# Single rows per step in a graph layer's gather: 80 by SP and 84 by ScalarE, instead of 76 by each

## The chip, the cores and the metric

The kernel runs on one core of a Trainium2 chip. The metric is the device time of one execution in microseconds (us). A core has five engines with instruction streams of their own: TensorE (PE in the profile), VectorE (DVE), ScalarE (ACT), GpSimd (POOL) and SyncE (SP). ACT, SP and POOL can also issue DMA transfers; the profile shows the issues as rows of ACTq, SPq and POOL.

## The reference

One layer of a graph network over 50,000 nodes with 128 features and 1,650,000 edges, sorted by destination. An edge has a type, 0 or 1, and each type has its own weight matrix and bias.

```
Xs    = X[src]
msg   = where(edge_type == 0, Xs @ W_data.T + b_data, Xs @ W_control.T + b_control)
agg   = segment_sum(msg, dst)
out   = relu(agg + X @ W_self.T + b_self)
x_new = layernorm(x + out)
```

All of it is computed in float32. The expensive part is `X[src]`: 1,650,000 rows of 512 bytes, in an order that only the input knows.

## The kernel before, in words

**Blocks and steps.** The edge list is cut into blocks. A block owns a window of nodes (B = 124) and has Q = 2 steps. The kernel sums the rows `X[src]` per destination and type first, and applies the weights afterwards, once per block. The sum is a product on TensorE: for up to 128 gathered rows, a 0/1 matrix `oh` made from the destinations and types says to which column each row is added.

**Three kinds of rows.** A step has R = 14 gathers of 128 rows, which POOL issues as indirect DMAs (function `gathers`, L551). Beside them it has S = 76 "single" rows: each is a plain DMA of 512 bytes whose address was loaded into a register (function `single_rows`). SP issues the single rows of a block's first step (q = 0), ACT those of its second step (q = 1). The registers are loaded up to LOAD = 28 at a time: 28, 28 and 20 (L580), and then come a register move and a DMA for each row (L585). F = 53 further edges a step fill places in the gathers' lists. So a block takes 14 x 2 x 128 + 2 x (53 + 76) = 3842 edges, and there are 430 blocks. The first and the last block are "plain": they have gathers alone. Single rows exist for blocks 1 to 428. The last block holds what is left over, 2050 edges in 17 gathers.

**What sets the order.** The order is written out by hand in the loop over blocks at the end of `straight`. In iteration b the single rows of block b + FAR (FAR = 4) are issued. They land in one of ten buffers (`y1`, five for each queue), so step q of block b + 4 can't start before TensorE has used step q of block b - 1. The gathers of a step land in one of SLOTS = 5 buffers. SP also stores each finished block (L691), loads the edge lists of ten blocks at a time (L196 to L200) and, for every eighth block, a window of transposed node features (L490). ACT also computes a square root for two blocks at once (L677).

**Marks.** Every queue sets 14 marks in a step's single rows, evenly spread: after row k it has set (k + 1) * 14 // 76 of them (L530, a semaphore that is counted up). `pace` holds POOL back by them: gather k of block b, from block 4 on, waits until queue k % 2 (0 is SP, 1 is ACT) has set k // 2 marks of its step for block b + 1 (LAG = 1). A block without single rows after it is not held back.

```
for k in ks:
    pace(b, k)
    ...
    copy = nc.gpsimd.indirect_dma_start(
```

**Products.** TensorE waits for a step's gathers (L558), multiplies them (L607), waits for the step's single rows (L611) and multiplies those in one more product (L613). DVE makes `oh`, counts, fills and the normalisation, and turns the single rows' indices into byte addresses (`offsets`, L191) for ten blocks at once.

Of the kernel before, what the change touches and what calls it, by code (L numbers as in the profile page):

```python
# [33 lines left out]
R = 14  # L34
W = 64
Q = 2
# [3 lines left out]
F = 53  # L40
LATE = 10
FX = LATE + F
R1 = R + 1
# [2 lines left out]
SIZES = [P] * R  # L46
SIZE = sum(SIZES)
CE = Q * SIZE
S = 76
LOAD = 28  # L50
BE = CE + Q * (F + S)
NBLK = 2 + (E + LATE - CE) // BE
REST = E + LATE - CE - (NBLK - 2) * BE
REST_ROWS = [min(n, max(0, REST - q * SIZE - sum(SIZES[:r]))) for q in range(Q) for r, n in enumerate(SIZES)]
# [28 lines left out]
TBL = GROUPS * GB  # L83
# [8 lines left out]
def plain(b):  # L92

    return b == 0 or b >= NBLK - 1
# [6 lines left out]
def straight(ctx, tc, c, x, x_t, edges_t, edges_f, edges_1, dst_first, first_p, out):  # L101
# [13 lines left out]
    nc = tc.nc  # L115
# [73 lines left out]
    def offsets(g):  # L189
        off = eds.tile([GB * Q, S], I32, name="off")  # L190
        nc.vector.tensor_scalar(off, one_g.pop(g), float(ROW), float((N - 1) * ROW), op0=ALU.mult, op1=ALU.min)  # L191
        off_g[g] = off

    def load_edges(g):
# [3 lines left out]
        nc.sync.dma_start(f.rearrange("b m f -> b (m f)"), edges_f[g * GB:(g + 1) * GB, :])  # L198
        one = eds.tile([GB * Q, S], I32, name="sd1", bufs=1)
        nc.sync.dma_start(one, edges_1[g * GB * Q:(g + 1) * GB * Q, :])  # L200
# [249 lines left out]
    def chunks_of(b, q):  # L450

        n = RCH if b == NBLK - 1 else C if b < NBLK else 0
        return range(q * R, max(q * R, min((q + 1) * R, n)))

    def column(k):
        return k // R * R1 + k % R

    def steps_of(b):
        return [q for q in range(Q) if len(chunks_of(b, q))]
# [12 lines left out]
    ys, ohs, cnts, accs, xTs, pos, hs, mvs, sds, os_ = {}, {}, {}, {}, {}, {}, {}, {}, {}, {}  # L472
# [54 lines left out]
    issued_no, asked, marks = [0] * Q, [0] * Q, {}  # L527

    def mark(q):
        (nc.scalar if q else nc.sync).sem_inc(issued[q], 1)  # L530
        issued_no[q] += 1
# [12 lines left out]
    def gathers(b, ks):  # L544
        i = pass_no[0] % SLOTS
        pass_no[0] += 1
        y = gat.tile([P, R, D], F32, name="y")
        for k in ks:
            pace(b, k)
            r = REST_ROWS[k] if b == NBLK - 1 else SIZES[k % R]  # L550
            copy = nc.gpsimd.indirect_dma_start(  # L551
                out=y[:r, k % R, :].bitcast(U8), out_offset=None, in_=x_rows,
                in_offset=bass.IndirectOffsetOnAxis(ap=idxs[b][:r, column(k):column(k) + 1], axis=0))
            copy.then_inc(landed[i], 16)
            tc.no_tile_sem_insts.add(copy.ins.name)
            tc.add_to_no_dep_group(f"rows{b}_{ks[0]}", copy.ins)
        seen[i] += 16 * len(ks)
        wait = nc.tensor.wait_ge(landed[i], seen[i])  # L558
        tc.declare_fence(wait.ins, group=f"rows{b}_{ks[0]}")
        return y  # L560
# [3 lines left out]
    got = [0] * ALONE  # L564
# [3 lines left out]
    def single_rows(b):  # L568
        if plain(b):
            return  # L570
        g, i = divmod(b, GB)
        for q in range(Q):
            j = alone_no[0] % ALONE
            alone_no[0] += 1
            marks[b, q] = issued_no[q]
            y = one.tile([S, D], F32, name="y1")
            for s0 in range(0, S, LOAD):
                n = min(LOAD, S - s0)
                at = i * Q + q
                _, regs = nc.values_load_multi_w_load_instructions(  # L580
                    off_g[g][at:at + 1, s0:s0 + n], engines=[ACT if q else SP], min_val=0, max_val=(N - 1) * ROW,
                    skip_runtime_bounds_check_because=CLAMPED)
                for k, r in enumerate(regs):
                    r = nc.s_assert_within(r, 0, (N - 1) * ROW, skip_runtime_bounds_check_because=CLAMPED)
                    copy = (nc.scalar if q else nc.sync).dma_start(y[s0 + k:s0 + k + 1, :].bitcast(U8),  # L585
                                               x_bytes[bass.ds(r, ROW)].rearrange("(p e) -> p e", e=ROW))
                    copy.then_inc(alone[j], 16)
                    tc.no_tile_sem_insts.add(copy.ins.name)
                    tc.add_to_no_dep_group(f"single{b}_{q}", copy.ins)
                    while issued_no[q] - marks[b, q] < (s0 + k + 1) * R // S:  # L590
                        mark(q)
            got[j] += 16 * S
            singles[b, q] = y, alone[j], got[j]

    def products(b, q, ks):
        of_step = chunks_of(b, q)
        if b == NBLK - 1:
            ys[b, q] = gathers(b, ks)
        elif ks[0] == of_step[0]:
            ys[b, q] = gathers(b, of_step)  # L600
        y = ys[b, q]
        if ks[0] == 0:
            accs[b] = ps.tile([P, Q, 3, W], F32, name="acc")
        acc = accs[b][:, q]
        for k in ks:
            r = REST_ROWS[k] if b == NBLK - 1 else SIZES[k % R]
            nc.tensor.matmul(acc[:, :2, :].rearrange("p t w -> p (t w)"), y[:r, k % R, :], ohs[b][:r, column(k), :],  # L607
                             start=k == of_step[0], stop=k == of_step[-1] and plain(b))
        if ks[-1] == of_step[-1] and not plain(b):
            y, landed_1, n = singles.pop((b, q))  # L610
            wait = nc.tensor.wait_ge(landed_1, n)  # L611
            tc.declare_fence(wait.ins, group=f"single{b}_{q}")
            nc.tensor.matmul(acc[:, :2, :].rearrange("p t w -> p (t w)"), y, ohs[b][:S, q * R1 + R, :], start=False, stop=True)  # L613
        if ks[-1] == of_step[-1] and q == steps_of(b)[-1]:
            for t in range(2):
                nc.tensor.matmul(accs[b][:, :q + 1, 2, :], to_row[:, t, :], cnts[b][:, :q + 1, t * W:(t + 1) * W],  # L616
                                 start=t == 0, stop=t == 1)
# [107 lines left out]

    columns(0)
    single_rows(1)
    spread(1)
    fill(1)
# [13 lines left out]
    for b in range(2, FAR):  # L743
        single_rows(b)
    made, fresh = 2, [2]
    ready = []
    for b in range(NBLK):
# [23 lines left out]
        if b == NBLK - 1:  # L771
            layer(b - 1)
            moments(b - 1)
            root(pair(b - 1))
            own_part(b)
            store(pair(b - 1))
            for done in pair(b - 1):
                store_rows(done)
            for step, ks in passes_of(b):
                if ks:  # L780
                    products(b, step, ks)
            break
# [3 lines left out]
        if b + FAR < NBLK:  # L786
            single_rows(b + FAR)
        for q, (step, ks) in enumerate(passes_of(b)):
            if ks:
                products(b, step, ks)  # L790
# [28 lines left out]
    b = NBLK - 1  # L819
# [340 lines left out]
```

## Time and profile before

| | |
|---|---|
| median of 3 runs | 15066.82 us (15066.48 to 15069.68) |
| the profiled execution, its own time | 15065.38 us |
| its span, first to last instruction | 15063.7 us |
| busy: PE, DVE, POOL | 39%, 80%, 76% of the span |
| POOL's gathers | 12012 + 17 |
| single rows on SP and on ACT | 32528 each |
| mean DMA rate | 61 GB/s |

Busy shares leave out register moves, semaphore instructions and DMA issues on SP and ACT. In the groups' rows, the part before the bar names line, engine, operation, tiles, shapes and count; then come busy time in us and the mean of one in ns; then the engine's idle time just before them and what ended most of it. In the waits' rows stand the total in us, how often, and the longest. In the timeline's rows stand the start in us from the span's start and the duration of a merged group of like instructions, with their count after the x; in brackets is the idle time before it.

### The profile page before, as it was taken

Reading aid. Unit: us, or ns where it says so; the run is one execution under the profiler, and the core shown is the slowest. Engines: PE = TensorE matmul, PEld = TensorE weight load, DVE = VectorE, ACT = ScalarE, POOL = GpSimd, SP = SyncE. Lnnn points to the kernel's source line nnn. Section 1 sums busy time; section 2 is a strip of 40 time slices with the busy share of each in tenths; the row PEclk is TensorE's granted clock in tenths of the full one; section 3 lists DMA queues with packets and bytes.
Section 4 is the critical chain, followed back from the end, with each engine's and each line's share of the span. In section 5 each row is a group of like instructions: output and inputs, shape, how many; then the busy total and the mean of one; then the engine's idle time right before and its main releaser. Section 6 shows DMA issues by size and latency. Waiting matters only on the chain. (4 is left out here: it accounts for less than half of the span.)

```text
span 15063.7 us, 244090 instructions
## 1 busy us (share of the span) xinstructions
PE 5857.4 (39%) x32862; PEld 5479.9 (36%) x32863; DVE 12073.6 (80%) x11957; ACT 67.2 (0%) x222; POOL 11376.7 (76%) x12039
## 2 busy tenths in 40 slices
PE   3433333333333333333333333333333333333333
PEld 3333333333333333333333333333333333333333
DVE  9878888877877788888888887878788888887875
ACT  0000000000000000000000000000000000000000
POOL 7777777777777777777777777777777777777777
PEclk7666666666666666666666666666666666666666
DMA  2222222222222222222222222222222222222222
GB/s 64 60 62 60 61 61 60 62 60 61 62 60 60 62 60 60 62 60 60 61 60 60 63 60 60 61 60 62 60 60 62 60 60 61 60 61 62 60 59 57
DMA packets 588595, 914.45 MB, mean 61 GB/s; under 512 B 262747, under 2 KB 381952, under 8 KB 586944
## 3 DMA queue, kind: packets, MB, share of 16 engines
q0 software_dynamic: 384928, 789.04, 20.8%
q1 hardware_dynamic: 136522, 92.72, 2.4%
q10 hardware_dynamic: 65494, 16.98, 0.6%
q14 instruction: 1384, 11.34, 0.2%
q8 instruction: 267, 4.37, 0.1%
HBM read 870.39 MB, written 27.30 MB: 60 GB/s over the span
## 5 line engine op out<-in xcount | busy, mean ns | idle before, releaser
L551 POOL DMA_INDIRECT y<-in_x,idx x12012 | 11359.3, 946 | 3667.3 <-issue 3075.1
L607 PE MATMUL acc<-oh,y 128*128 128x128 f32 x24058 | 4774.6, 384 | 8916.1 <-PEq L558 8871.1
L607 PEld LDWEIGHTS acc<-oh,y 128*128 128x128 f32 x24058 | 4571.4, 293 | 9247.8 <-issue 5053.0
L515 DVE TENSOR_REDUCE cnt<-oh 128x256 bf16<-128x3840 f32 x430 | 2834.7, 6592 | 14.7
L507 DVE TENSOR_TENSOR oh<-col,small 128x3840 f32<-128x3840 f32 x430 | 1781.5, 4143 | 0.0
L416 DVE TENSOR_REDUCE by<-new 128x126 bf16<-128x1890 f32 x428 | 1497.0, 3498 | 14.6
L621 DVE TENSOR_TENSOR sums<-acc,sums 128x192 f32 x860 | 307.3, 357 | 1341.1 <-PE acc L616 1292.9
L395 DVE COPY small<-cb 128x30 f32<-128x30 f32 x428 | 82.0, 192 | 1219.7 <-PE small L423 1219.7
L400 DVE TENSOR_TENSOR new<-m,small 128x1890 f32<-128x1890 f32 x428 | 909.0, 2124 | 14.7
L397 DVE TENSOR_TENSOR m<-rk,small 128x1890 f32<-128x1890 f32 x428 | 908.9, 2124 | 14.6
L404 DVE TENSOR_REDUCE v_new<-new 128x30 f32<-128x1890 f32 x428 | 907.9, 2121 | 14.7
L413 DVE TENSOR_TENSOR new<-m,small 128x1890 f32<-128x1890 f32 x428 | 905.8, 2116 | 0.0
L613 PE MATMUL acc<-oh,y 76*128 76x128 f32 x1712 | 334.0, 276 | 0.0
L651 PE MATMUL po<-wmsgT,sums 128*124 128x128 f32 x1720 | 304.5, 300 | 0.0
L613 PEld LDWEIGHTS acc<-oh,y 76*128 76x128 f32 x1712 | 265.6, 195 | 0.0
L641 PE MATMUL po<-own_w,xT 128*124 128x256 f32 x860 | 262.3, 386 | 0.8 <-DVE h L657 0.8
L637 DVE TENSOR_TENSOR sums<-pl,sums 128x372 f32<-128x372 f32 x428 | 233.2, 545 | 14.9
L651 PEld LDWEIGHTS po<-wmsgT,sums 128*124 128x124 f32 x1720 | 221.5, 188 | 53.0 <-issue 1.6
L448 DVE TENSOR_TENSOR pl<-pl,xT 128x248 f32<-128x248 f32 x428 | 181.7, 425 | 46.6 <-DVE xT L501 2.7
L649 PE MATMUL po<-bias,sums 3*124 3x128 f32 x860 | 208.3, 322 | 1.2 <-DVE sums L621 1.2
L649 PEld LDWEIGHTS po<-bias,sums 3*124 3x124 f32 x860 | 125.2, 183 | 149.3 <-issue 147.4
L501 DVE COPY xT<-xw 128x124 f32 x430 | 111.7, 260 | 77.4 <-issue 74.2
(147 smaller groups left out, 2915.1 us busy)
## 6 DMA issues: line engine op xcount, KB each, us to landing
y<-in_x SPq DMA_DIRECT2D x32528, 0.5 KB
y<-in_x ACTq DMA_DIRECT2D x32528, 0.5 KB
y<-in_x,idx POOLq DMA_INDIRECT x12012
xw<-in_x_t SPq DMA_DIRECT2D x54, 496.0 KB
out<-o SPq DMA_DIRECT2D x430, 62.0 KB
sdt<-in_edges_t SPq DMA_DIRECT2D x43, 450.0 KB
sdt_f<-in_edges_f SPq DMA_DIRECT2D x43, 14.8 KB
sd<-in_edges SPq DMA_DIRECT2D x43, 5.9 KB
```

Source lines behind the costliest of these rows:

```text
L397: nc.vector.tensor_tensor(m, rk_g[g][:, i, :, None].to_broadcast([P, C1, FX]), rank_no_ps[:, None, :].to_broadcast([P, C1, FX]), op=ALU.is ...
L400: nc.vector.tensor_tensor(new.rearrange("p (q r) f -> p q r f", r=R1), m.rearrange("p (q r) f -> p q r f", r=R1), vf.rearrange("p (q f) -> ...
L404: nc.vector.tensor_reduce(v, new, AX.X, ALU.add)
L413: nc.vector.tensor_tensor(old, m, cb[:, :, None].to_broadcast([P, C1, FX]), op=ALU.mult)
L416: nc.vector.tensor_reduce(by, old.rearrange("p (q r) f -> p q f r", r=R1), AX.X, ALU.add)
L507: nc.vector.tensor_tensor(oh, col_g[g][:, i, :, None].to_broadcast([P, C1, 2 * W]), num_ps[:, None, :].to_broadcast([P, C1, 2 * W]), op=AL ...
L515: nc.vector.tensor_reduce(cnt, ohs[b].rearrange("p (q r) w -> p q w r", r=R1), AX.X, ALU.add)
L551: copy = nc.gpsimd.indirect_dma_start(out=y[:r, k % R, :].bitcast(U8), out_offset=None, in_=x_rows, in_offset=bass.IndirectOffsetOnAxis(ap ...
L607: nc.tensor.matmul(acc[:, :2, :].rearrange("p t w -> p (t w)"), y[:r, k % R, :], ohs[b][:r, column(k), :], start=k == of_step[0], stop=k = ...
L613: nc.tensor.matmul(acc[:, :2, :].rearrange("p t w -> p (t w)"), y, ohs[b][:S, q * R1 + R, :], start=False, stop=True)
L649: nc.tensor.matmul(po, a[0:3, 2, :B], bias, start=False, stop=False)
L651: nc.tensor.matmul(po, a[:, t, :B], c["wmsgT"][:, t * D:(t + 1) * D], start=False, stop=t == 1)
```

## The change

The number of single rows becomes one for each step, SINGLE = (80, 84): 80 in a block's first step, on SP, and 84 in its second, on ACT. Each step still loads its registers in three loads, 28, 28 and 24 on SP, 28, 28 and 28 on ACT, and each still sets 14 marks. The buffer of a step has room for 84 rows, and the product takes as many of them as were filled. A block takes 3584 + 106 + 164 = 3854 edges, so there are 429 blocks, and the last one has 768 edges in 6 gathers, all of its first step. The host lays out the edge list to match.

```diff
-S = 76
-LOAD = 28
-BE = CE + Q * (F + S)
+SINGLE = (80, 84)
+LOADS = (28, 28)
+S = max(SINGLE)
+BE = CE + Q * F + sum(SINGLE)
...
-            for s0 in range(0, S, LOAD):
-                n = min(LOAD, S - s0)
+            for s0 in range(0, SINGLE[q], LOADS[q]):
+                n = min(LOADS[q], SINGLE[q] - s0)
...
-                    while issued_no[q] - marks[b, q] < (s0 + k + 1) * R // S:
+                    while issued_no[q] - marks[b, q] < (s0 + k + 1) * R // SINGLE[q]:
                         mark(q)
-            got[j] += 16 * S
+            got[j] += 16 * SINGLE[q]
...
-            nc.tensor.matmul(acc[:, :2, :].rearrange("p t w -> p (t w)"), y, ohs[b][:S, q * R1 + R, :], start=False, stop=True)
+            nc.tensor.matmul(acc[:, :2, :].rearrange("p t w -> p (t w)"), y[:SINGLE[q], :], ohs[b][:SINGLE[q], q * R1 + R, :], start=False, stop=True)
```

More of the change, by code (lines that the diff above doesn't have):

```diff
@@ L1122 @@
         rest = a[CE:].reshape(TBL - 1, BE)
-        steps = rest.reshape(TBL - 1, Q, SIZE + S + F)
+        step_at = [sum(SIZE + s + F for s in SINGLE[:q]) for q in range(Q)]
         cols = np.full((TBL, Q, R1, P), pad, np.int32)
@@ L1127 @@
             cols[0, :, r, :n] = a[:CE].reshape(Q, SIZE)[:, at:at + n]
-            cols[1:, :, r, :n] = steps[:, :, at:at + n]
+            for q in range(Q):
+                cols[1:, q, r, :n] = rest[:, step_at[q] + at:][:, :n]
             cols[NBLK - 1, :, r, :n] = rest[NBLK - 2, :CE].reshape(Q, SIZE)[:, at:at + n]
-        cols[1:NBLK - 1, :, R, :S] = steps[:NBLK - 2, :, SIZE:SIZE + S]
+        for q, n in enumerate(SINGLE):
+            cols[1:NBLK - 1, q, R, :n] = rest[:NBLK - 2, step_at[q] + SIZE:][:, :n]
         if k == "src":
@@ L1133 @@
         fills = np.full((TBL * Q, FX), pad, np.int32)
-        own = steps[:NBLK - 2, :, SIZE + S:].reshape((NBLK - 2) * Q, F)
+        own = np.stack([rest[:NBLK - 2, step_at[q] + SIZE + n:][:, :F] for q, n in enumerate(SINGLE)], 1).reshape(-1, F)
         fills[Q:(NBLK - 1) * Q, LATE:] = own
```

## The prediction

> **What bounds the kernel now.** I read the page's costliest groups first, for an engine that has no slack, then the waits of that engine, then its timeline.
>
> ```profile
> span 15063.7 us, 244090 instructions
> PE 5857.4 (39%) x32862; PEld 5479.9 (36%) x32863; DVE 12073.6 (80%) x11957; ACT 67.2 (0%) x222; POOL 11376.7 (76%) x12039
> L551 POOL DMA_INDIRECT y<-in_x,idx x12012 | 11359.3, 946 | 3667.3 <-issue 3075.1
> ...
> POOL y L551 <- issue: 3079.1, 10088, 0.3
> POOL y L551 <- ACTq L530: 254.6, 834, 0.3
> POOL y L551 <- SPq L530: 228.4, 748, 0.3
> ...
> 7000.10 0.94 POOL L551 DMA_INDIRECT y<-in_x,idx  x1 [0.30 <-issue]
> 7001.35 0.94 POOL L551 DMA_INDIRECT y<-in_x,idx  x1 [0.31 <-SPq L530]
> ...
> 15048.96 0.88 POOL L551 DMA_INDIRECT y<-in_x,sdt  x1 [0.30 <-issue]
> ```
>
> By busy share DVE (80%) stands above POOL (76%), but POOL has no idle time that is a wait: each of its gathers takes 0.94 us, 0.30 us passes before the next, and the longest idle time before one is 0.3 us, whoever is named as the releaser. So POOL runs gather after gather from start to end. There are 28 x 429 + 17 = 12029 of them, from about 3 us to 15048.96: 15046 / 12028 = 1.249 us each, 28 x 1.249 = 34.97 us a block. That is the period everything else must stay under. The last gather ends at 15049.8, and 13.9 us of work follow.
>
> ACT and SP look empty (ACT 0%), because DMA issues are not counted as busy. But POOL's gathers wait on marks that these queues set, so how full the queues are has to be read from their timelines. First ACT's queue, in three stretches: before any result is stored, early, and late.
>
> ```profile
> 80.44 30.27 ACTq L585 DMA_DIRECT2D y<-in_x  x76
> ...
> 145.42 0.47 ACTq L585 DMA_DIRECT2D y<-in_x  x1
> ...
> 408.33 63.71 ACTq L585 DMA_DIRECT2D y<-in_x  x152
> 472.22 0.29 ACT L677 ACTIVATE sd<-mv,eps 124x2 f32<-124x2 f32 x1 [65.72 <-issue]
> 474.33 65.80 ACTq L585 DMA_DIRECT2D y<-in_x  x152
> 540.31 0.29 ACT L677 ACTIVATE sd<-mv,eps 124x2 f32<-124x2 f32 x1 [67.80 <-issue]
> ...
> 676.06 24.02 ACTq L585 DMA_DIRECT2D y<-in_x  x57
> ...
> 13070.36 0.29 ACT L677 ACTIVATE sd<-mv,eps 124x2 f32<-124x2 f32 x1 [69.80 <-PEq L558]
> 13078.23 62.26 ACTq L585 DMA_DIRECT2D y<-in_x  x152
> ```
>
> 152 rows are two steps of 76. From 408.33 to 676.06 ACT does eight steps, 33.47 us each, and after each ACTIVATE the next row comes 2.1 us later. Late, the row after the ACTIVATE comes 7.6 us later (13070.66 to 13078.23): there ACT waits. So early ACT runs freely at 33.47 us a step, gains 34.97 - 33.47 = 1.5 us a block on POOL, and stops gaining once it is as far ahead as its ten row buffers let it be. From 80.44 to 145.42 are two quieter steps, 32.49 us each. ACT's whole reserve is therefore 1.5 us a block in the busy stretch and 2.5 us in the quiet one.
>
> SP's queue, early and late, and the wait that holds it back late:
>
> ```profile
> 371.33 29.90 SPq L585 DMA_DIRECT2D y<-in_x  x76
> 401.45 0.28 SPq L691 DMA_DIRECT2D out<-o  x1
> 403.91 30.05 SPq L585 DMA_DIRECT2D y<-in_x  x76
> ...
> 671.78 28.29 SPq L585 DMA_DIRECT2D y<-in_x  x70
> ...
> 13087.69 0.28 SPq L691 DMA_DIRECT2D out<-o  x1
> 13094.17 29.91 SPq L585 DMA_DIRECT2D y<-in_x  x76
> ...
> SPq L585 <- PE acc L613: 803.6, 340, 4.0
> ```
>
> From 371.33 to 671.78 SP does nine steps, 33.38 us each, its store of a block's result included. Late it waits for PE to release a row buffer: 803.6 us in all.
>
> **The change part by part.** A block takes 3584 + 106 + 164 = 3854 edges instead of 3842. That leaves 429 blocks, and the last has 768 edges, six gathers instead of 17. *Removed:* POOL issues 28 x 428 + 6 = 11990 gathers, 39 fewer; at 1.249 us that is 48.7 us off the engine that sets the end now. The edges do not vanish: they become eight more rows on ACT and four more on SP in every block.
>
> What a row and a register load cost on ACT, from one quiet step:
>
> ```profile
> 103.86 6.85 ACTq L585 DMA_DIRECT2D y<-in_x  x20
> L585 ACTq DMA_DIRECT2D y<-in_x x32528: 227/228/617, 15.3 to 14891.8; - x200
> ...
> L580 ACTq TENSOR_LOAD <-off x1: 1949/1949/1949, 90.1 to 90.1; - x1
> L580 ACTq TENSOR_LOAD <-off x1: 1538/1538/1538, 102.2 to 102.2; - x1
> ```
>
> Twenty rows took 6.85 us, the first of them 0.47 us as in the row at 145.42; the others (6.85 - 0.47) / 19 = 0.336 us each, register move and marks included. Bounds: 0.32 with the marks taken out (their number, 14 a step, stays), 0.36 if the busy stretch's slower rows are added. Eight rows: 2.7 us (2.6 to 2.9). The third load of a step brings 20 registers in 1.54 us now, the second 28 in 1.95 us. With 84 rows all three bring 28, so the third grows by 0.41 us. Together ACT's step grows by 3.1 us (3.0 to 3.3).
>
> Of loads, the Trainium skill ("DMA: Bandwidth & Descriptors", Latency and other measured facts) says that a `tensor_load` has a floor of about 600 ns, and names no slope. If a load cost a flat sum, the term of 0.41 us would be nothing and the step 3.1 - 0.4 = 2.7 us longer; the two loads above differ with their width, so I keep the term.
>
> SP's step grows by 4 x 0.336 and, for 24 registers instead of 20, half of 0.41 us: 1.55 us. Freely running that is 33.38 + 1.55 = 34.9 us, just under POOL's 34.97: SP by itself would still keep up.
>
> ACT would not: 33.47 + 3.1 = 36.6 us a step by the busy stretch, 32.49 + 3.1 = 35.6 by the quiet one, and both are over 34.97. The cover that hid ACT's issues is used up by 0.6 to 1.6 us a block. What is late next is POOL: a gather of block b with odd number waits for a mark of ACT's step for block b + 1. At the start there is no lead to live on. Block 4, the first with these waits, begins on POOL after 112 gathers, at about 143 us, and ACT's step 5 began at 145.42. So ACT paces POOL from block 4 to block 426, and a block lasts as long as ACT's step.
>
> Between 35.6 and 36.6 I take 36.0. Early, SP's rows follow its store by 2.46 us (401.45 to 403.91) and rows on both queues are slower; late, SP waits and they follow by 6.5 us (13087.69 to 13094.17). With ACT as the bound, SP, needing 34.9 or less, soon runs as far ahead as its buffers go and waits a little over a microsecond after each store. That is less than late in the kernel before, so part of the slowness should stay.
>
> The sum: ACT's first row of step 5 stood at 145.42 us; four steps grown by 3.1 put it at 157.8. Steps 5 to 427 are 423 periods. Their last odd gather is released some 4.3 us before the end of the last period (the next step's load that isn't there, 2.3, and the rows behind the last but one mark, 2.0). After it POOL has one gather of block 426, 28 of 427 and 6 of 428, which wait for no mark: 35 x 1.249 = 43.7. Then the 13.9 us of the end, and the 1.7 us that the profiled execution (15065.4 us) had outside its span: 157.8 + 423 x 36.0 - 4.3 + 43.7 + 13.9 + 1.7 = 15440.8 us. In general 212.8 + 423 x step. The profiled execution lies 1.4 us below the median of the runs, which is nothing here.
>
> Costed at nothing: the rows' products on PE and the scaling of the offsets on DVE.
>
> ```profile
> L613 PE MATMUL acc<-oh,y 76*128 76x128 f32 x1712 | 334.0, 276 | 0.0
> L607 PE MATMUL acc<-oh,y 128*128 128x128 f32 x24058 | 4774.6, 384 | 8916.1 <-PEq L558 8871.1
> L191 DVE TENSOR_SCALAR off<-sd 20x76 int32<-20x76 int32 x43 | 8.0, 187 | 0.1
> ```
>
> A product of 76 rows takes 0.276 us against 0.384 for 128 rows, so 84 rows cost at most 0.11 more; PE idles 8916 us in front of its gathers' products. The scaling runs 43 times at 0.19 us, eight columns more, on a DVE that POOL does not wait for. Uncovered, both would be under 0.5 us a block.
>
> **The rivals.** *POOL stays the bound* (the other side: faster). Only the 39 gathers count: 15065.4 - 48.7 = 15016.7 us. It decides if ACT's step of 84 stays at 34.97 or less. For it: POOL never waits for ACT today, and late ACT idles visibly. Against it: eight rows and the wider load would have to cost 1.5 us (busy) or 2.5 us (quiet) instead of 3.1.
>
> *The step lands within 0.1 us of POOL's period*: the lost and the won time cancel, about 15065 us, a step of 35.1. Nothing but chance speaks for it.
>
> *ACT as quiet as before the first store*: 35.25 to 35.7 (the low end is 32.49 + 8 x 0.32 + half of the load's 0.41), so at 35.6 the end is 212.8 + 423 x 35.6 = 15272 us. For it: the late stretch of the kernel before, where 152 rows take 62.26 us with waits inside. *ACT as busy as from 408 to 676 us throughout*: 212.8 + 423 x 36.6 = 15695 us. For it: in that stretch ACT also ran without a wait, which is what it will do.
>
> *One descriptor generator for both queues.* If a row held something shared for all of its 0.228 us, a block's 164 rows would need 37.4 us and the end would be 212.8 + 423 x 37.4 = 16033 us. Against it: 152 rows at 0.228 are 34.7 us, yet both queues did a step in 33.4 us, loads included, so rows overlap. The Trainium skill ("Perfetto Trace Analysis", DMA Instruction — HWDGE) says that the generator is locked for exclusive use within the profiled time of such a DMA; by these rows the lock can hold only a part of it.
>
> **How the numbers follow.** ACT's step between 35.7 and 36.4 us: 0.48, at 36.0, 15441 us. Quiet, 35.25 to 35.7: 0.25. Busy, 36.4 to 36.9: 0.14. Shared generator: 0.03. POOL stays the bound: 0.08. Cancelled: 0.02. The range takes the quiet and the busy case in, from a step of 35.25 (15124) to 36.65 (15716). Within 0.2%, 30 us, a run can't be told from no change. Faster 0.08, same 0.02, slower 0.90.
>
> **What would show it.** If I am right, POOL's waits for ACT's marks (254.6 us in all, longest 0.3) become several hundred microseconds with single ones of some microseconds. The row after every ACTIVATE comes about 2 us later, late in the run too. SP still waits for PE at its rows. The last ACT row, 157 us ahead of the last gather before (14891.8 to 15048.96), comes some 45 us ahead of it. 28 gathers take 36 us in mid-run. I am wrong if POOL's longest wait stays at 0.3 us and the last gather starts near 15000 us; the slope is wrong if ACT's rows, freely running, take other than 0.32 to 0.36 us or its 28-register loads other than 1.95 us.

## The result, and the profile after

The changed kernel takes 36,611.95 us (median of 4 runs, 36,607.55 to 36,614.29) against 15,066.65 us before: 2.43 times as long, 95% interval 2.4258 to 2.4342. The forecast was 15,441 us.

The costliest groups on the page of the changed kernel:

```profile
span 36612.5 us, 357556 instructions
L991 POOL DMA_INDIRECT y<-table,idx x14000 | 14921.6, 1066 | 5919.8 <-issue 2757.7
L994 PE MATMUL pa<-y,oh 128*125 128x128 f32 x28000 | 11037.7, 497 | 7973.5 <-DMA y<-table,idx 7938.8
L552 POOL DMA_INDIRECT y<-in_x,idx x11984 | 11323.0, 945 | 4191.5 <-issue 2990.2
```

The gathers of before are there, now as L552. Two of the three costliest groups did not exist before: 14,000 gathers from a `table` and 28,000 products. They belong to a function `general`, which computes the whole layer a second time, from a table of messages per node. The kernel has always held it, behind a branch that the text above has not spoken of. `find_bad` finds, on the chip, whether anything in the input doesn't fit the fast layout, and the branch asks for what it found:

```
nc.vector.tensor_scalar(bad[:, 2:3], latest, float(LATE), None, op0=ALU.is_gt)
nc.vector.tensor_scalar(bad[:, 0:1], mm[:, 0:1], 0.0, None, op0=ALU.is_lt)
nc.vector.tensor_scalar(bad[:, 1:2], mm[:, 1:2], float(W), None, op0=ALU.is_ge)
...
found = nc.values_load(bad, min_val=0, max_val=4 * P,
...
with tc.If(found > 0):
    ...
    general(own, tc, c, x, src, dst, etype, out)
```

The third line is the one that matters here: a step's destinations have to lie within W = 64 nodes, counted from the step's first one (0 to 63 above it). Where the one computation ends and the other begins is in the timeline of POOL, and the share of each in the table by stage (busy time of each engine, then TensorE's granted clock, DMA share and GB/s):

```profile
15523.19 0.94 POOL L552 DMA_INDIRECT y<-in_x,sdt  x1 [0.30 <-issue]
15530.19 0.24 POOL L851 IOTA node<- 128x125 f32 x1 [6.06 <-PE po L652]
...
0.00:15534.00 15534.00, 6034.14 (x32765) 5451.42 (x32766) 12045.14 (x11933) 66.74 (x221) 11333.93 (x12006) 0.64 0.28 59
15534.00:36612.00 21078.00, 11582.59 (x30373) 7324.99 (x30373) 2872.24 (x3883) 188.53 (x646) 14941.98 (x14014) 0.51 0.20 52
```

So the first computation, the one that the forecast is about, ends near 15,534 us, and 21,078 us come on top. In the first one the waits, the issues and ACT's timeline look like this:

```profile
POOL y L552 <- ACTq L531: 873.4, 1218, 2.2
POOL y L552 <- SPq L531: 258.8, 846, 0.7
...
L586 ACTq DMA_DIRECT2D y<-in_x x35868: 234/235/610, 15.9 to 15480.8; - x200
L581 ACTq TENSOR_LOAD <-off x1281: 1875/2012/2214, 13.8 to 15469.1; - x183
...
448.82 70.20 ACTq L586 DMA_DIRECT2D y<-in_x  x168
...
669.46 30.48 ACTq L586 DMA_DIRECT2D y<-in_x  x72
...
13132.68 0.29 ACT L678 ACTIVATE sd<-mv,eps 124x2 f32<-124x2 f32 x1 [72.44 <-issue]
13134.78 70.04 ACTq L586 DMA_DIRECT2D y<-in_x  x168
```

POOL now waits for ACT's marks: 873.4 us in all, up to 2.2 us at once. Before, no idle time that the profile put down to ACT's marks was longer than the 0.3 us that pass between any two gathers. After the end of the ACTIVATE the next row comes 1.8 us later, late in the run too (13132.97 to 13134.78; before it was 7.6 us). From the first to the last row ACT does 427 steps in 15,465 us, 36.2 us each. It sets the pace.

### The profile page after: what moved, and what is told of

It is laid out like the page before. It is cut to its first block, busy times and chain, and to the rows that moved or that the text cites. A ratio compares the mean times of both kernels' runs of the same rounds, so it can differ in the third digit from the quotient of the medians.

```text
span 36612.5 us, 357556 instructions
## 1 busy us (share of the span) xinstructions
PE 17616.7 (48%) x63138; PEld 12776.4 (35%) x63139; DVE 14917.4 (41%) x15816; ACT 255.3 (1%) x867; POOL 26275.9 (72%) x26019
## 5 line engine op out<-in xcount | busy, mean ns | idle before, releaser
L991 POOL DMA_INDIRECT y<-table,idx x14000 | 14921.6, 1066 | 5919.8 <-issue 2757.7
L994 PE MATMUL pa<-y,oh 128*125 128x128 f32 x28000 | 11037.7, 497 | 7973.5 <-DMA y<-table,idx 7938.8
L552 POOL DMA_INDIRECT y<-in_x,idx x11984 | 11323.0, 945 | 4191.5 <-issue 2990.2
L994 PEld LDWEIGHTS pa<-y,oh 128*125 128x125 f32 x28000 | 6916.8, 308 | 12088.2 <-DMA y<-table,idx 11608.3
L608 PEld LDWEIGHTS acc<-oh,y 128*128 128x128 f32 x23980 | 4355.2, 282 | 9649.1 <-issue 8223.5
L1013 DVE TENSOR_TENSOR acc<-pa,bself 125x128 f32<-125x128 f32 x400 | 116.7, 292 | 17208.3 <-PE pa L994 17208.3
L608 PE MATMUL acc<-oh,y 128*128 128x128 f32 x23980 | 4646.7, 375 | 3461.6 <-PEq L559 3460.9
L516 DVE TENSOR_REDUCE cnt<-oh 128x256 bf16<-128x3840 f32 x429 | 2869.6, 6689 | 14.6
L987 DVE TENSOR_TENSOR oh<-rel,node 128x4375 f32<-128x4375 f32 x400 | 1883.3, 4708 | 1.7
L387 PE MATMUL small<-v_f,row_of 74*128 74x126 bf16 x427 | 106.8, 251 | 3097.5 <-DVE at L431 3061.1
L417 DVE TENSOR_REDUCE by<-new 128x126 bf16<-128x1890 f32 x427 | 1498.5, 3509 | 14.6
L684 DVE RECIPROCAL rstd<-sd 124x2 f32<-124x2 f32 x215 | 35.7, 166 | 3076.9 <-ACT sd L678 3076.9
L398 DVE TENSOR_TENSOR m<-rk,small 128x1890 f32<-128x1890 f32 x427 | 907.2, 2125 | 14.6
L401 DVE TENSOR_TENSOR new<-m,small 128x1890 f32<-128x1890 f32 x427 | 907.0, 2124 | 14.7
L405 DVE TENSOR_REDUCE v_new<-new 128x30 f32<-128x1890 f32 x427 | 906.1, 2122 | 14.7
L1007 PE MATMUL px<-ident,x_g 125*128 125x125 f32 x400 | 139.3, 425 | 1207.1 <-DMA t<-in_edge_type 458.8
L614 PE MATMUL acc<-oh,y 80*128 80x128 f32 (+1 forms) x1708 | 405.0, 326 | 0.0
```

Of the source, the lines that this page charges most:

```text
L398: nc.vector.tensor_tensor(m, rk_g[g][:, i, :, None].to_broadcast([P, C1, FX]), rank_no_ps[:, None, :].to_broadcast([P, C1, FX]), op=ALU.is ...
L401: nc.vector.tensor_tensor(new.rearrange("p (q r) f -> p q r f", r=R1), m.rearrange("p (q r) f -> p q r f", r=R1), vf.rearrange("p (q f) -> ...
L405: nc.vector.tensor_reduce(v, new, AX.X, ALU.add)
L417: nc.vector.tensor_reduce(by, old.rearrange("p (q r) f -> p q f r", r=R1), AX.X, ALU.add)
L516: nc.vector.tensor_reduce(cnt, ohs[b].rearrange("p (q r) w -> p q w r", r=R1), AX.X, ALU.add)
L552: copy = nc.gpsimd.indirect_dma_start(out=y[:r, k % R, :].bitcast(U8), out_offset=None, in_=x_rows, in_offset=bass.IndirectOffsetOnAxis(ap ...
```

## The experiments

Two things had to be told apart: what started the second computation, and whether the first one by itself behaves as forecast. Counting over the input's destinations, with 3854 edges a block, finds edges outside in one place only: the last eleven of the edges that fill places in block 7's first step all go to one node, 64 above the step's first node, where 63 is the last that fits. (The expectations below speak of one edge; it is one node, with eleven edges.) With 3842 edges there is none. All other conditions hold in both. That count was made off the chip; the runs test it.

**Moving the edges by 50 places.** Empty places at the end of the first block's list shift all later blocks by 50 edges. By the count no edge is outside then.

```diff
+PADS = 50
...
+        a = np.concatenate([a[:CE - PADS], np.full(PADS, pad, np.int32), a[CE - PADS:]])
```

> The changed kernel with 50 empty places put at the end of the first block's list, so that every later block begins 50 edges later; the instructions stay the same but for one gather more in the last block. Theory A (one filled edge of block 7 lies 64 nodes above its step's first node, the check for the 64-node window counts it, and the whole layer is computed a second time): no edge lies outside now, so 15,525 to 15,555 us, the 15,533 us at which the first computation ends in the changed kernel and little else. Theory B (another check trips, or the second computation has another cause): 36,612 us as before.

Measured: 20,034 us, beside 19,464 us for the kernel before in the same set of runs: ratio 1.0301 (1.0284 to 1.0319). The second computation is gone, there is no L991 in the profile. But the kernel before was 4,400 us slower than it had been. The waits and issues of this run show where (last, the register moves of the kernel before in the first profile):

```profile
POOL y L553 <- SPq L532: 4297.7, 2012, 5.2
...
L587 SPq MOVE y<-in_x x34160: 2/29/1403, 15.8 to 19925.1; - x200
...
7029.73 43.19 SPq L587 DMA_DIRECT2D y<-in_x  x80
...
L585 SPq MOVE y<-in_x x32528: 29/29/37, 15.2 to 14874.6; - x200
```

A register move on SP takes 29 ns at the median and at most 37 ns in the first profile; here single ones take up to 1,403 ns, and 80 rows of SP take 43 us instead of 31 to 32. Both queues stood still at times, at any instruction. Below, "standing queues" means this. In such a set a ratio says what an edit does to the second computation, but the price of rows can't be read from it.

**The kernel before, with its edges moved by 34 places.** By the count this puts two edges of block 7 at 64 nodes there too.

> The kernel before, 76 rows in both steps, with 34 empty places put at the end of the first block's list; by the input, a filled edge of block 7 then lies 64 nodes above its step's first node. Theory A: the second computation runs here too, 15,067 + (36,612 - 15,533) = 36,146 us, between 36,120 and 36,170. Theory B (it takes 80 and 84 rows): 15,067 us.

Measured in the same set, in one run: 42,210 us, 22,745 us more than the kernel before, where 21,079 us more were expected; the queues stood in this run too. The second computation runs, with 76 rows in both steps:

```profile
L991 POOL DMA_INDIRECT y<-table,idx x14000 | 14748.5, 1053 | 7776.4 <-issue 3462.0 <-remote 1347.6 <-DMA s<-in_src 1089.5
...
POOL y L552 <- SPq L531: 4163.0, 2116, 6.8
```

So it doesn't take 80 and 84 rows; it takes edges outside the window.

**The check's limit at 65 nodes.** One constant of the changed kernel is another:

```diff
-nc.vector.tensor_scalar(bad[:, 1:2], mm[:, 1:2], float(W), None, op0=ALU.is_ge)
+nc.vector.tensor_scalar(bad[:, 1:2], mm[:, 1:2], float(W + 1), None, op0=ALU.is_ge)
```

> The changed kernel with one constant changed: the check for the window counts an edge as outside from 65 nodes on instead of 64. It leaves out that one edge's proper column (it is added for the wrong type). Theory A: 15,525 to 15,550 us. Theory B, another check: 36,612 us.

Measured in the same set, in one run: 20,000.9 us beside 19,464 us, and no second computation. So no other condition of `find_bad` was met, and no edge lies further out than 64. With the two runs above, that settles the cause of the factor 2.43.

> The changed kernel with the window check's limit at 65 nodes instead of 64 and nothing else, sent alone; it leaves out the proper column of one edge. The first computation of the changed kernel ended at 15,533 us of its trace. If that is what it takes by itself, 15,525 to 15,555 us beside a kernel before of 15,067 us, ratio 1.031, and POOL's waits for ACT's marks as in the changed kernel (873 us in all). If the added rows cost nothing once the second computation is gone: 15,018 us. If the queues stand still in the kernel before too: about 1.02 to 1.03 of it.

The same kernel in a later set without standing queues, beside a kernel before of 15,072 us: 15,535.4 us (15,531 to 15,544), ratio 1.031 (1.0293 to 1.0327). This is the first computation by itself. Its waits, issues, last gathers and the ACT queue, early and late:

```profile
span 15529.7 us, 253706 instructions
...
POOL y L552 <- ACTq L531: 793.1, 1042, 2.5
SPq L586 <- PE acc L614: 378.9, 152, 3.6
...
L586 ACTq DMA_DIRECT2D y<-in_x x35868: 227/228/631, 15.9 to 15470.5; - x200
L552 POOL DMA_INDIRECT y<-in_x,sdt x6: 940/943/945, 15506.9 to 15513.1; - x6
...
445.58 70.33 ACTq L586 DMA_DIRECT2D y<-in_x  x168
...
664.66 34.24 ACTq L586 DMA_DIRECT2D y<-in_x  x84
...
13053.54 71.04 ACTq L586 DMA_DIRECT2D y<-in_x  x168
...
13271.61 3.45 ACTq L586 DMA_DIRECT2D y<-in_x  x10
```

Six steps from 445.58 to 664.66 take 36.5 us each, six from 13053.54 to 13271.61 take 36.3; over all 427 steps it is 36.2.

**68 rows by SP, 84 by ACT.** The blocks, the 12,029 gathers and the edges per block are those of the kernel before.

```diff
-SINGLE = (80, 84)
+SINGLE = (68, 84)
```

> 68 rows by SP and 84 by ACT: 3842 edges a block as in the kernel before, so the same 430 blocks and 12029 gathers; eight rows only change queues. If ACT's step of 84 rows sets the pace: 212.8 + 424 x step + 11 x 1.249, which is 15,279 us at 35.5 us a step (SP, with fewer rows, waits longer after its stores and leaves ACT's rows quiet) and 15,533 us at 36.1 (ACT's rows as slow as in the changed kernel, whatever SP does). If POOL stays the bound: 15,067 us.

> 68 rows by SP, 84 by ACT, the blocks and gathers of the kernel before. Without the stalls: 15,279 us if ACT's step falls to 35.5 us with SP waiting longer after its stores, 15,533 us if it stays at 36.1 us whatever SP does, 15,067 us if ACT's rows don't set the pace at all.

Both of these were measured with standing queues: 1.0206 (1.0181 to 1.023) and 1.0237 (1.0217 to 1.0258) of the kernel before.

> 68 rows by SP and 84 by ACT again, with the blocks and gathers of the kernel before. In the last two sets of runs the queues of SP and ACT stood still for 0.7 us and more at a time, in the kernel before as well (19,464 and 19,632 us). If the kernel before takes 15,067 us here: 15,279 us if ACT's step falls to 35.5 us because SP waits longer after its stores, 15,533 us if ACT's step stays at 36.1 us whatever SP does, 15,067 us if ACT doesn't set the pace. If the queues stand still here too, about 1.02 to 1.03 of the kernel before.

> 68 rows by SP and 84 by ACT once more: the earlier run gave 15,254 us in its profiled execution and 15,506 us in its other one. If SP's waiting after its stores settles how slow ACT's rows are, and either course can set in, single executions fall near 15,254 us (ACT's step 35.4 us) or near 15,506 us (36.0 us), and in a trace of the second kind SP's first row follows its store sooner than in a trace of the first (9 us and 2.5 us by turns there). If 15,506 us was a single disturbance: all near 15,254 us.

In two sets without standing queues the kernel before took 15,066 and 15,083 us, and this one 15,254 us, then 15,247 to 15,304 us (ratio of the second set 1.0131, 1.011 to 1.0151). In each of the two sets one further execution took 15,506 and 15,503 us; what it did inside is not known, because the traces kept are of 15,254 and 15,247 us, so the question of the last expectation stays open. In the first of these POOL, ACT and SP did this:

```profile
POOL y L552 <- ACTq L531: 455.9, 946, 1.6
...
13058.88 68.72 ACTq L586 DMA_DIRECT2D y<-in_x  x168
...
13270.90 4.33 ACTq L586 DMA_DIRECT2D y<-in_x  x12
...
7034.97 0.28 SPq L692 DMA_DIRECT2D out<-o  x1
7044.37 26.73 SPq L586 DMA_DIRECT2D y<-in_x  x68
```

Six steps from 13058.88 to 13270.90: 35.3 us each, a microsecond less than above with the same 84 rows on ACT; over the whole run it is 35.4 against 36.2. SP has twelve rows fewer. Here it waits up to 9.4 us after its store before its next row, but that is no difference: the mean from store to next row is 4.0 us in both traces. What differs is ACT's rows right after SP's store. From 400 us on, and with the register loads left out, they start 0.380 us apart on the mean in the first 10 us after a store beside 80 rows of SP, and 0.345 beside 68; in the remaining time it is 0.347 in both. Some 20 rows of a step fall into those 10 us, so this makes 0.7 of the 0.8 us. Moving eight rows from SP to ACT thus costs 1.3%, with not one gather saved or added: POOL was no longer what set the end.

**The changed kernel with its edges moved, again.**

> The changed kernel with 50 empty places at the end of the first block's list once more, on another chip. In the first run both it and the kernel before had queues that stood for 0.7 or 1.4 us at a time, at any instruction of SP and ACT; POOL waited for SP's marks there. If those stalls belong to that chip and are absent here: the kernel before at 15,067 us and this one at 15,525 to 15,555 us, POOL's gathers waiting for ACT's marks. If they come with the edit: 20,000 us beside 15,067.

> The changed kernel with 50 empty places at the end of the first block's list. If the kernel before takes 15,067 us here: 15,525 to 15,555 us by theory A (only the window check started the second computation, and ACT's step of 36.1 us sets the pace of the first); 15,015 us if the eight rows cost nothing once the check holds. If the queues stand still as in two earlier sets: 1.02 to 1.03 of the kernel before.

> The changed kernel with 50 empty places at the end of the first block's list, sent alone. The kernel before took 15,066 us in the two sets with one other kernel and 19,460 to 19,630 us in the three sets with three or four others, so I expect it at 15,066 us here. Then this one is at 15,525 to 15,555 us (1.031 of it) if the window check alone brought the second computation and ACT's step of 36.1 us sets the pace of the first; at 15,015 us if the added rows cost nothing.

> The changed kernel with 50 empty places at the end of the first block's list. Where the kernel before takes 15,066 us: 15,525 to 15,555 us, 1.031 of it, if only the second computation goes and ACT's step of 36.1 us sets the pace; 15,015 us if the added rows cost nothing. Where the queues stand still and the kernel before takes over 19,400 us: about 20,040 us, as in the earlier runs.

All four were measured with standing queues, the last two although no other changed kernel was in the set: 20,064, 20,052, 20,041 and 20,057 us beside 19,632, 19,628, 19,446 and 19,640 us, ratios 1.0223, 1.0213, 1.0312 and 1.0217. They repeat that the second computation is gone and say no more about the rows. The price had to come from the kernel with the limit at 65.

**78 rows on both queues.**

> 78 rows on both queues: 430 blocks, 3 gathers in the last, 12015 in all, no edge outside a window. ACT's step is 33.4 + 2 x 0.336 + 0.1 = 34.2 us and SP's 34.2 too, both under POOL's 34.97, so POOL sets the pace: 15,067 - 14 x 1.249 = 15,049 us. If a queue's step is over POOL's period after all, it is slower than 15,067.

> 78 rows on both queues, 14 gathers fewer, no edge outside a window; both queues' steps are worked out at 34.2 us against POOL's 34.97. If POOL sets the pace: 15,067 - 14 x 1.249 = 15,049 us, 0.999 of the kernel before. If the queues stand still: 1.006 of it.

Both were measured with standing queues: 1.0061 (1.0045 to 1.0078) and 1.0073 (1.0056 to 1.0089). Where the queues set the end in the kernel before, two more rows on each cost time.

> 78 rows on both queues, 14 gathers fewer, no edge outside a window, sent alone. Both queues' steps, worked out at 34.2 us, stay under POOL's 34.97: 15,067 - 14 x 1.249 = 15,049 us, 0.9988 of the kernel before. If the rows cost more than thought and a step is over 34.97: slower than 15,067.

Without standing queues: 15,058.3 us (15,056.5 to 15,059.8, 10 runs) beside 15,066.7 us, ratio 0.9995 (0.9985 to 1.0004). POOL keeps the bound, as the waits show:

```profile
span 15054.9 us, 247428 instructions
...
POOL y L552 <- ACTq L531: 272.0, 890, 0.5
POOL y L552 <- SPq L531: 238.2, 779, 0.6
...
15034.39 1.41 POOL L552 DMA_INDIRECT y<-in_x,sdt  x1 [0.30 <-issue]
15033.35 5.74 PE L608 MATMUL acc<-oh,y 128*128 128x128 f32 x28 [9.88 <-PEq L559]
15042.68 0.83 PE L608 MATMUL acc<-oh,y 128*128 128x128 f32 x6
```

The last gather starts 14.6 us earlier than before, of 17.5 that 14 gathers are worth. From there to the end it takes 20.5 us instead of 14.7: with three gathers in the last block, its products begin only at 15042.68, behind those of the block before, which begin at 15033.35. So 8.4 us are left, which can't be told from no change by the interval, though all ten executions lie below the thirteen of the kernel before (15,064.1 us and more). Of the versions tried it is the only one that was not slower, and only without standing queues.

**80 rows on both queues.** By the count no edge is outside here.

> 80 rows on both queues: 429 blocks, 20 gathers in the last, 12004 in all, and by the input no edge outside a window. ACT's step is 33.4 + 4 x 0.336 + 0.2 = 35.0 us in the busy stretch, less once SP waits; POOL's period is 34.97. If POOL sets the pace: 15,065 - 25 x 1.249 = 15,034 us. If ACT's step is 35.3: 15,156 us.

> 80 rows on both queues, 25 gathers fewer than before, no edge outside a window. If POOL sets the pace: 15,065 - 25 x 1.249 = 15,034 us. If ACT's step is 35.3 us: 15,156 us. If the queues stand still: 1.02 of the kernel before.

With standing queues the ratios were 1.0202 (1.0182 to 1.0222) and 1.0205 (1.0188 to 1.0222).

> 80 rows on both queues, 25 gathers fewer than before, no edge outside a window. With 78 on both, POOL still set the pace (15,058 us). If POOL does so here: 15,065 - 25 x 1.249 = 15,034 us. If ACT's step is 35.3 us, over POOL's 34.97: 15,156 us. Where the queues stand still: 1.02 of the kernel before.

Without them 15,187 us (15,165 to 15,189) beside 15,073 us, ratio 1.0076 (1.0059 to 1.0092). The waits and issues:

```profile
POOL y L552 <- SPq L531: 407.1, 988, 2.5
POOL y L552 <- ACTq L531: 271.9, 879, 0.8
...
L586 SPq DMA_DIRECT2D y<-in_x x34160: 227/228/659, 15.7 to 15083.8; - x200
L586 ACTq DMA_DIRECT2D y<-in_x x34160: 227/228/671, 15.8 to 15062.8; - x200
```

427 steps: 35.29 us on SP, 35.24 on ACT, both over POOL's 34.97. POOL's long waits are for SP. The point at which the queues take over lies between 78 and 80 rows on both.

## Why the prediction was wrong

**The step that failed** is the first sentence of the change part by part: "A block takes 3584 + 106 + 164 = 3854 edges instead of 3842." I took from it the number of blocks and gathers, and nothing else. But it also moves the edges on which every later block and step begins, and the fast layout holds only for inputs whose steps stay within 64 nodes. Eleven edges of 1,650,000, all of one node, came to lie one node outside, `find_bad` found them, and the layer was computed again: 21,078 us. In the sum it is the term behind the last gather, "the 13.9 us of the end": 21,088 us followed there (15524.1 to 36612.5). No rival covered this. The kernel's text showed the check and the branch. The profile before has the check's own rows (L698 to L712, some 0.6 us each or less), but no row of the second computation, since the branch was not taken. Whether anything would lie outside could be worked out from the input, and I didn't.

**The forecast of the first computation** was right in its mechanism; the numbers are those with the limit at 65. POOL's waits for ACT's marks came (793 us, longest 2.5 us; "several hundred microseconds with single ones of some microseconds"). ACT's row comes about two microseconds after the ACTIVATE's start throughout. (The prediction counts its 2.1 us from the ACTIVATE's start and its 7.6 us from the end.) SP still waited for PE. 28 gathers took 36.2 us on the mean, with 36 forecast. The last ACT row lies 43 us ahead of the last gather (15470.5 to 15513.1), with some 45 forecast. Its time by itself, 15,535 us, is 94 us over the 15,441 of the sum and inside its range.

**The term that was mis-sized** in that sum is the step, 36.0 us against 36.2 on the mean; 423 x 0.22 = 93 us. Early in the run six steps took 36.5 us each with the limit at 65 and 36.8 in the changed kernel (448.82 to 669.46), with 36.6 forecast for the busy stretch. With SP less loaded they took 35.3 late in the run (35.25 to 35.7 forecast for the quiet one). So the two ends were right, and the middle was chosen a little low. The price of the rows and of the wider load, 3.1 us, measured 36.5 - 33.5 = 3.0 us between the two early stretches, and 3.3 in the changed kernel, where a DMA issue on ACT took 235 ns at the median instead of 228. ACT's first row of step 5, put at 157.8 us, came at 157.89. A 28-register load took 2.01 us at the median against the 1.95 read from a single one. One division is off: 15046 / 12028 is 1.251, not 1.249, so a block of 28 gathers took 35.03 us on the mean; 1.249 us is the distance of most gathers. None of the comparisons here turns on that.

**SP's term** was too small: 34.9 us was forecast for 80 rows running freely, and 35.3 was measured with 80 on both. "SP by itself would still keep up" failed there: SP's rows waited for PE 1.5 us in all, and POOL waited for SP. In the changed kernel it was not put to the test, because ACT set the pace and SP waited.

**The rivals.** *POOL stays the bound* fell for the changed kernel and held for 78 rows. *One descriptor generator held for all of a row's time* would have made a block 37.4 us; it took 36.2. The Trainium skill ("Perfetto Trace Analysis", DMA Instruction — HWDGE) has the generator locked for exclusive use while a DMA's descriptors are made; no run here shows the lock itself. That ACT's 84 rows are slower beside 80 rows of SP than beside 68 looks like a part shared by the rows, but the traces speak against it: outside the 10 us after a store ACT's rows start 0.347 us apart beside either.

## What to carry to other kernels

Where a kernel has a fallback that depends on its input, ask of every edit that regroups the data whether the guard still holds, and work that out from the input before pricing anything: eleven edges outside, of 1,650,000, cost more here than the whole kernel before. An engine that shows 0% busy because it only issues DMAs can still be nearly full; its reserve per block is read from its timeline, in a stretch where it runs without a wait. With three engines within 5% of one another per block, a saving on the first is worth at most what is left on the next.

## What the runs showed of the hardware that was not expected

The queues of SP and ACT stood still in five sets of runs, for about 0.7 or 1.4 us at a time and at any instruction; the kernel before then took 19,410 to 19,659 us instead of 15,064 to 15,085. All five sets, and none of the six others, held the kernel with 50 empty places, also when no other changed kernel was in the set; one and the same chip gave both. Whether that kernel brings it about, and how, is open. Single register moves are recorded there with 2 ns, where none took under 29 before, so it may be the recording of the trace that stands still; that was not tried. In those sets the queues and not POOL set the end even with 76 rows on both (in the kernel before with its edges moved, 4,163 us of POOL's waits were for SP).

ACT's single rows depend on what SP does beside it: late in the run 84 rows took 36.3 us a step beside 80 rows on SP and 35.3 beside 68. By the traces the slow rows are those in the 10 us after SP's store, 0.380 us apart instead of 0.347. They are slow (0.37) even before SP has issued its next row, so it isn't SP's next rows that they wait for. Why the same store costs ACT nothing beside 68 rows is open, and no run changed the store by itself.
